# Softmax totals of the first attention layer: from 128x32 products in one bank to 64x64 products in two

## The chip, the cores and the metric

The kernel runs on one core of one Trainium2 chip. Its engines work side by side: TensorE (PE, with PEld for its weight loads), VectorE (DVE), ScalarE (ACT), GpSimd (POOL) and SyncE (SP), which here mostly issues transfers. [...] The metric is the device time of one execution in microseconds (us), as a median of several runs.

## The reference

The kernel computes two layers of attention over images, in fp32, for 8 images ("batches" here) of 512 channels and 32 x 32 = 1024 positions, with 8 heads of 64 channels. The part that matters is the first layer:

```python
x = x + L0(_gn(x))            # then a second attention layer on the result
# L0: group norm, then
qkv = einsum('oc,bct->bot', qkv_w, normed) + qkv_b
weight = einsum('bct,bcs->bts', q, k)          # q, k scaled by 64 ** -0.25
weight = softmax(weight, axis=-1)
a = einsum('bts,bcs->bct', weight, v)
out = einsum('oc,bct->bot', proj_w, xf + a) + proj_b
```

The second layer (head mixing, softmax, instance norm over each head's map) is not touched by the change.

## The kernel before

The kernel does layer 0 for all eight batches and then layer 1. The order of the instructions on each engine is the order in which the program writes them. Small pieces of work are put between the others with an `Agenda`: `ag.at(slot, fn)` files a function under a slot, and the main loop runs the slots as it comes to them.

In layer 0, each batch has projections for k, v and q (`project0`, matmuls at L899, in 128x128 of the PE array), then `attention0`, then the output projection. `attention0` works on 64 steps i = 0 to 63: 8 groups g of 8 steps. A group is one pair of heads (m = 0, 1) and one half of the queries (512 columns); a step is a block of 128 keys. The loop goes forward by two steps at a time:

- `scores(i)` (L1081): four products of 64x64 weights with 512 columns give the scores, keys on partitions, into two PSUM banks; then ACT takes the exponential into the tile `e` (L1086; 7 buffers).
- `values(i)` (L1107), two steps behind: four products of 64x64 with 512 columns. Keys 0 to 63 (a = 0) and keys 64 to 127 (a = 1) go to separate banks, the two heads to the halves of each bank. At the end of a group ACT copies the two banks out (`u`, L1118).
- `sums(i)` (L1092 and L1094): DVE adds the exponentials of the group into `zacc`, which still has 128 partitions of partial sums.
- Then come three stages of the softmax's division: `totals(g)` two slots after the group's last values, `reciprocals(g)` six slots after, `finish(g)` ten slots after.

`totals` adds `zacc` over its 128 partitions with products against ones (L1126), which also repeat each result over many partitions. ACT copies the result to SBUF (`row`, L1131), and a transfer on SP's queue spreads it over all 128 partitions, 8 values on each (`zc`, L1133). `reciprocals` adds the halves of `u` (L1137), inverts `zc` (L1140), sends the inverse to DRAM (L1142) and reads it back spread over the partitions (`rzb`, L1145). It also collects two numbers for a check of the range. `finish` multiplies `u` by `rzb` and adds it into `xa` (L1161, L1163).

Two more things have a part in this. PSUM has eight banks: layer 0 gives four to the score tiles (tag `s`), two to tag `a0`, one to `a1` and one to `small`. The tag `small` has one buffer and serves the group norm's statistics of the next batch, through `small_psum`. In batches 0 to 6 their first matmul (`gs.means`, L619, tile `pm`) is filed under slot 43, the second (`gs.squares`, L630, tile `pv`) under slot 45, and the reading of `pv` (`scale`) under slot 47:

```python
agenda.at(slot + 23, gs.means)      # slot = 20
agenda.at(slot + 25, gs.squares)
agenda.at(slot + 27, scale)
```

In batch 7 the statistics for layer 1 over batches 0 to 6 take the same bank, under slots 22, 25 and 28; the last of them begins with DVE's reading of `pv` (L634). With the loop's numbers, the totals of group g run in slot 8g + 10; those of group 7 run after the loop, behind the next projection's k (`ag.flush()`).

Of the kernel before, what the change touches and what calls it, by code (L numbers as in the profile page):

```python
# [9 lines left out]
F32 = mybir.dt.float32  # L10
# [8 lines left out]
P = 128  # L19
# [448 lines left out]
def tile_two_attention_layers(  # L468
# [19 lines left out]
    nc = tc.nc  # L488
    B, C, T = x_d.shape
    H = w_head.shape[0]  # L490
    D = C // H
    NCC = C // P
    NT = T // P
    FB = 512
# [21 lines left out]
    def const_tile(name, shape, dt=F32):  # L516
        return const.tile(shape, dt, tag=name, name=name)
# [13 lines left out]
    ones = const_tile("ones", [P, P])  # L531
# [162 lines left out]
    with ExitStack() as l0:  # L694
# [4 lines left out]
        zpool = l0.enter_context(tc.tile_pool(name="zpool", bufs=2))  # L699
        stat = l0.enter_context(tc.tile_pool(name="stat", bufs=2))  # L700
        ps_s = l0.enter_context(tc.tile_pool(name="ps_s", bufs=2, space=PSUM))
        ps_a = l0.enter_context(tc.tile_pool(name="ps_a", bufs=1, space=PSUM))

        def small_psum(nm):
            return ps_a.tile([P, FB], F32, tag="small", name=nm)
# [363 lines left out]
        def attention0(b, agenda):  # L1069
            q, k, v = q_t[b], k_t[b], v_t[b]  # L1070
            e, acc, u, zacc, zc, rzb = {}, {}, {}, {}, {}, {}
# [46 lines left out]
                        nc.scalar.copy(u[g][a], acc[g][a])  # L1118

            def totals(g):  # L1120


                HB = FB // 2
                z = ps_a.tile([P, FB], F32, tag="a0", name=f"z_{b}_{g}", bufs=2)[:, :HB]
                for c in range(4):
                    nc.tensor.matmul(  # L1126
                        z[c * 32 : c * 32 + 32], ones[:, :32], zacc[g][:, c // 2, ts(c % 2, HB)],
                        start=True, stop=True, tile_position=(0, c * 32),
                    )
                row = zpool.tile([P, HB], F32, tag="row", name=f"row0_{b}_{g}")  # L1130
                nc.scalar.copy(row, z)  # L1131
                zc[g] = stat.tile([P, T // P], F32, tag="zc", name=f"zc_{b}_{g}")
                nc.sync.dma_start(out=zc[g], in_=row[0::32])  # L1133

            def reciprocals(g):

                nc.vector.tensor_add(u[g][0], u[g][0], u[g][1])  # L1137
                zs = zc[g]
                rz = stat.tile([P, T // P], F32, tag="rz0", name=f"rz_{b}_{g}")
                nc.vector.reciprocal(rz, zs)  # L1140
                zd = dram.tile([2, FB], F32, tag=f"zd0_{b}_{g}", name=f"zd0_{b}_{g}")
                nc.sync.dma_start(out=zd, in_=rz)  # L1142
                rzb[g] = zpool.tile([P, FB], F32, tag="rzb", name=f"rzb_{b}_{g}")
                for m in range(2):
                    nc.sync.dma_start(  # L1145
                        out=rzb[g][m * D : m * D + D], in_=zd[m].partition_broadcast(D)
                    )
                col = b * H + g
                junk = stat.tile([P, T // P], F32, tag="junk0", name=f"junkz_{b}_{g}")
                nc.vector.tensor_scalar(  # L1150
                    junk, zs, 1.0, 0.0, ALU.mult, ALU.add, accum_out=chk[:, 1, col : col + 1]
                )
                r2 = stat.tile([P, T // P], F32, tag="r20", name=f"r2_{b}_{g}")
                nc.vector.scalar_tensor_tensor(
                    r2, rz, 1.0 / RZ_MAX, rz, ALU.mult, ALU.mult,
                    accum_out=chk[:, 0, col : col + 1],
                )
# [8 lines left out]
            for i in range(0, NI + 2, 2):  # L1166
                if i < NI:
                    scores(i)
                    scores(i + 1)
                if i >= 2:  # L1170
                    for w in (i - 2, i - 1):
                        values(w)
                        sums(w)
                    if (i - 1) % NG == NG - 1:
                        g = (i - 1) // NG
                        agenda.at(i + 2, lambda g=g: totals(g))
                        agenda.at(i + 6, lambda g=g: reciprocals(g))
                        agenda.at(i + 10, lambda g=g: finish(g))
                agenda.run(i)
                agenda.run(i + 1)  # L1180
# [83 lines left out]
    with ExitStack() as l1:  # L1264
# [5 lines left out]
        zpool = l1.enter_context(tc.tile_pool(name="zpool1", bufs=1))  # L1270
        stat = l1.enter_context(tc.tile_pool(name="stat1", bufs=2))
        ps_a = l1.enter_context(tc.tile_pool(name="ps1_a", bufs=2, space=PSUM))
# [619 lines left out]
        for b in range(B):  # L1892
            more = b + 1 < B
            a = Attention1(b)
# [143 lines left out]
```

## Time and profile before

| | us |
|---|---|
| median of three runs | 4051.75 |
| their range | 4051.15 to 4058.64 |
| profiled execution | 4059.13 |
| its span, first to last instruction | 4057.0 |
| PE busy | 3927.5 |
| DVE busy | 2834.4 |
| ACT busy | 1969.0 |
| POOL busy | 128.7 |

Layer 0 takes the time up to about 1750 us, layer 1 the rest. The mean granted clock of TensorE is 0.993 of full speed. In the profile, a row names the source line, the engine, the operation, the tiles (written <- read) and the shapes, then how many there were; a number in square brackets is how long the engine had been idle, with what ended that. A logical fp32 matmul is two matmuls in the trace, and matmuls in different parts of the PE array overlap.

### The profile page before, as it was taken

What the parts mean: (1) busy time and instruction counts of PE and PEld (TensorE: products, weight loads), DVE (VectorE), ACT (ScalarE), POOL (GpSimd) and SP (SyncE); (2) the same over time, 40 slices, a digit from 0 to 9 for tenths busy, and PEclk for the clock granted to TensorE, in tenths of its full rate; (3) what the DMA queues carried; (4) which work ended last, traced back from release to release, by engine and by line L of the source; (5) the groups of instructions that cost most, each with busy time, mean ns of one, the idle gap of its engine ahead of it and who ended that gap; (6) DMA issues with size and microseconds to landing.
All of it is one profiled execution on the core that took longest, in us unless ns stands there. A gap on an engine that the chain in (4) does not pass through costs nothing. (4 is left out here: it accounts for less than half of the span.)

```text
span 4057.0 us, 96037 instructions
## 1 busy us (share of the span) xinstructions
PE 3927.5 (97%) x41932; PEld 1817.7 (45%) x41932; DVE 2834.4 (70%) x4124; ACT 1969.0 (49%) x2431; POOL 128.7 (3%) x150
## 2 busy tenths in 40 slices
PE   8999999999999999999999999999999999999997
PEld 4353535353444435334444534544444444445344
DVE  4748475756666575748849859769679679498596
ACT  1727263545445363516617427347257166174273
POOL 0000000000000000000000001001000000000010
PEclk9999999999999999999999999999999999999998
DMA  3313131211111111228738639559469287386384
GB/s 124 114 47 115 45 118 48 87 50 59 60 66 66 68 53 60 77 83 208 182 120 220 189 105 234 155 143 231 128 174 233 78 216 194 114 223 193 104 212 121
DMA packets 268636, 519.12 MB, mean 128 GB/s; under 512 B 49840, under 2 KB 84912, under 8 KB 261552
## 3 DMA queue, kind: packets, MB, share of 16 engines
q1 hardware_dynamic: 261664, 497.96, 42.9%
q0 software_dynamic: 6544, 14.94, 1.6%
q8 instruction: 331, 5.42, 0.6%
q14 instruction: 97, 0.79, 0.1%
HBM read 197.16 MB, written 46.92 MB: 60 GB/s over the span
## 5 line engine op out<-in xcount | busy, mean ns | idle before, releaser
L1687 DVE STREAM_TRANSPOSE et<-e 128x2048 f32<-128x2048 f32 x256 | 586.7, 2292 | 133.8 <-ACT e L1675 127.6
L1714 PEld LDWEIGHTS a<-et,v 128*64 128x64 f32 x16384 | 509.4, 138 | 287.2 <-issue 215.8
L1698 DVE BATCH_NORM_STATS2 bn<-e 128x6 f32<-128x512 f32 x1024 | 633.5, 673 | 0.0
L1086 ACT ACTIVATE e<-s 128x1024 f32<-128x1024 f32 x512 | 497.2, 1026 | 233.9 <-PE s L1081 233.4
L1675 ACT ACTIVATE e<-m 128x1024 f32<-128x1024 f32 x512 | 496.3, 1021 | 208.4 <-issue 102.1
L1643 ACT COPY raw<-s 128x1024 f32<-128x1024 f32 x480 | 475.0, 1019 | 229.6 <-PE s L1631 193.1
L1714 PE MATMUL a<-et,v 128*64 128x64 f32 x16384 | 557.3, 225 | 5.8 <-DVE et L1687 5.1
L1631 PE MATMUL s<-k,q 64*64 64x512 f32 x4096 | 541.7, 615 | 9.7 <-DVE q L1497 3.1
L1094 DVE TENSOR_TENSOR zacc<-zacc,e 128x1024 f32<-128x1024 f32 x384 | 468.8, 1221 | 93.8 <-ACT e L1086 71.8
L1081 PE MATMUL s<-q,k 64*64 64x512 f32 x4096 | 490.1, 593 | 2.3 <-ACT e L1086 2.3
L1107 PE MATMUL a<-e,v 64*64 64x512 f32 x4096 | 484.1, 589 | 0.0
L1665 PE MATMUL m<-re,wmix 32*32 32x512 f32 x8192 | 334.9, 611 | 72.6 <-DMA re<-raw 60.7
L1107 PEld LDWEIGHTS a<-e,v 64*64 64x64 f32 x4096 | 156.7, 133 | 282.8 <-issue 282.5
L1081 PEld LDWEIGHTS s<-q,k 64*64 64x64 f32 x4096 | 147.9, 133 | 275.2 <-issue 240.7
L1631 PEld LDWEIGHTS s<-k,q 64*64 64x64 f32 x4096 | 118.0, 132 | 259.2 <-issue 85.0
L1458 PE MATMUL pv<-wv,y 128*128 128x512 f32 x480 | 212.1, 597 | 0.0
L1730 ACT COPY q<-a 64x256 f32<-64x256 f32 x256 | 93.7, 366 | 158.9 <-PE a L1714 156.3
L1665 PEld LDWEIGHTS m<-re,wmix 32*32 32x32 f32 x8192 | 71.6, 103 | 215.5 <-ACT raw L1643 88.3
L1763 POOL DMA_DIRECT2D zd<-rz x56 | 34.7, 619 | 3492.5 <-DMA y<-x 1858.2
L1458 PEld LDWEIGHTS pv<-wv,y 128*128 128x128 f32 x480 | 89.3, 190 | 117.4 <-issue 109.5
L1462 ACT COPY v<-pv 128x512 f32<-128x512 f32 x30 | 17.6, 585 | 218.4 <-PE pv L1458 218.4
L1092 DVE TENSOR_TENSOR zacc<-e,e 128x1024 f32<-128x1024 f32 x64 | 78.3, 1223 | 55.3 <-ACT e L1086 55.3
(315 smaller groups left out, 3936.8 us busy)
## 6 DMA issues: line engine op xcount, KB each, us to landing
re<-raw SPq DMA_DIRECT2D x1024, 256.0 KB
left_q<-left_q SPq DMA_DIRECT2D x17, 1792.0 KB
left_p<-left_p SPq DMA_DIRECT2D x17, 1792.0 KB
left_k<-left_k SPq DMA_DIRECT2D x10, 1792.0 KB
x<-in_x_dram SPq DMA_DIRECT2D x32, 512.0 KB
rzb<-zd SPq DMA_DIRECT2D x128, 128.0 KB
x<-x SPq DMA_DIRECT2D x64, 256.0 KB
left_v<-left_v SPq DMA_DIRECT2D x8, 1792.0 KB
```

Source lines behind the costliest of these rows:

```text
L1081: nc.tensor.matmul(ps[c * D : c * D + D, m], k[r, hp, k0 : k0 + D], q[r, hp, ts(f, FB)], start=True, stop=True,)
L1086: nc.scalar.activation(e[i], ps, AF.Exp, scale=S0 * S0)
L1094: nc.vector.tensor_add(zacc[g], zacc[g], e[i])
L1107: nc.tensor.matmul(acc[g][a][m * D : m * D + D], v[rows, kc, ts(2 * hp + m, D)], e[i][rows, m], start=(kc == 0), stop=(kc == NG - 1),)
L1458: nc.tensor.matmul(ps[:, m], y_t[b][:, c, ts(2 * i + m, P)], w[:, c], start=(c == 0), stop=(c == NCC - 1),)
L1631: nc.tensor.matmul(ps[c * D : c * D + D, m], qo_t[b][r, p, hp, ts(c, D)], k_t[b][r, hp, ts(kh, FB)], start=True, stop=True,)
L1643: nc.scalar.copy(dst, ps)
L1665: nc.tensor.matmul(ps[a // 2][c * 32 : c * 32 + 32, a % 2].rearrange("p (r kb k) -> p r kb k", r=2, k=32), wmix[rows].rearrange("p g i -> ...
L1675: nc.scalar.activation(e[:, :, 2 * h : 2 * h + 2].rearrange("p r a k -> p a r k"), ps[h].rearrange("p a (r k) -> p a r k", r=2), AF.Exp,)
L1687: nc.vector.transpose(self.et[p, u].rearrange("p kb (r st a) g q -> p st kb r (a g q)", r=2, st=2)[:, st], self.e[p, s].rearrange("p r a ( ...
L1698: nc.vector.bn_stats(self.bn[p][:, s, a], e[:, :, a].rearrange("p r k -> p k r"))
L1714: nc.tensor.matmul(acc[two * D : two * D + D, s].rearrange("p (x q) -> p x q", q=4), v_t[b][:, kb, ts(g, D)], et[:, kb, :, g], start=(kb = ...
```

## The change

The products of `totals` become four of 64x64 weights with 512 columns: per key half a and head m one, the halves in separate banks, a = 0 in a bank of tag `a0` as before and a = 1 in the bank of tag `small`. So each total arrives as two halves. Two copies on ACT, of 128x512 each, take the place of one of 128x256; two transfers take the place of one; `row` has one buffer of 2 x 512 columns instead of two of 256; and DVE adds the two halves of `zc`, 128x8 elements, ahead of the reciprocal.

```diff
             def totals(g):
-                HB = FB // 2
-                z = ps_a.tile([P, FB], F32, tag="a0", name=f"z_{b}_{g}", bufs=2)[:, :HB]
-                for c in range(4):
-                    nc.tensor.matmul(
-                        z[c * 32 : c * 32 + 32], ones[:, :32], zacc[g][:, c // 2, ts(c % 2, HB)],
-                        start=True, stop=True, tile_position=(0, c * 32),
-                    )
-                row = zpool.tile([P, HB], F32, tag="row", name=f"row0_{b}_{g}")
-                nc.scalar.copy(row, z)
-                zc[g] = stat.tile([P, T // P], F32, tag="zc", name=f"zc_{b}_{g}")
-                nc.sync.dma_start(out=zc[g], in_=row[0::32])
+                z = [ps_a.tile([P, FB], F32, tag="a0", name=f"z_{b}_{g}", bufs=2), small_psum(f"zs_{b}_{g}")]
+                for a in range(2):
+                    rows = slice(a * D, a * D + D)
+                    for m in range(2):
+                        nc.tensor.matmul(
+                            z[a][m * D : m * D + D], ones[rows, :D], zacc[g][rows, m],
+                            start=True, stop=True,
+                        )
+                row = zpool.tile([P, 2, FB], F32, tag="row", name=f"row0_{b}_{g}", bufs=1)
+                zc[g] = stat.tile([P, 2, T // P], F32, tag="zc", name=f"zc_{b}_{g}")
+                for a in (1, 0):
+                    nc.scalar.copy(row[:, a], z[a])
+                    nc.sync.dma_start(out=zc[g][:, a], in_=row[0::D, a])

             def reciprocals(g):
                 nc.vector.tensor_add(u[g][0], u[g][0], u[g][1])
-                zs = zc[g]
+                zs = zc[g][:, 0]
+                nc.vector.tensor_add(zs, zs, zc[g][:, 1])
                 rz = stat.tile([P, T // P], F32, tag="rz0", name=f"rz_{b}_{g}")
```

## The prediction

> **What bounds the kernel.** I read the page's busy times first, then windows one softmax group long, then the timelines of the places where the totals are made. The profiled execution took 4059.13 us, 4057.0 of them span; the median of the runs shown is 4051.75, lower by 7.4 us, about their own spread (4051.15 to 4058.64). I make the sum against the profile and add it to the median.
>
> ```profile
> PE 3927.5 (97%) x41932; PEld 1817.7 (45%) x41932; DVE 2834.4 (70%) x4124; ACT 1969.0 (49%) x2431; POOL 128.7 (3%) x150
> ```
>
> ```profile
> 129.96:144.42 14.46, 14.46 (x141) 4.95 (x137) 9.19 (x14) 11.55 (x17) 0.00 (x0) 1.00 0.37 147
> 329.57:344.04 14.47, 14.47 (x141) 4.96 (x137) 14.09 (x23) 9.82 (x12) 0.00 (x0) 1.00 0.24 77
> ```
>
> Each window runs from one totals matmul to the next (length, then PE, PEld, DVE, ACT busy): PE is busy throughout, DVE 9.2 to 14.1, ACT 9.8 to 11.6 of 14.5 us. So the first layer's attention is paced by PE. What lengthens PE's stream there counts in full; ACT, DVE and DMA count only if they make PE wait.
>
> A busy PE says little about the price of an instruction, so I take prices from starts:
>
> ```profile
> 113.67 1.90 PE L1107 MATMUL a<-e,v 64*64 64x512 f32 x16
> 115.49 0.64 PE L1126 MATMUL z<-zacc,ones 128*32 128x256 f32 x8
> 116.06 1.95 PE L1081 MATMUL s<-q,k 64*64 64x512 f32 x16
> 117.83 1.90 PE L1107 MATMUL a<-e,v 64*64 64x512 f32 x16
> 119.55 1.90 PE L1081 MATMUL s<-q,k 64*64 64x512 f32 x16
> 121.26 1.04 PE L1107 MATMUL a<-e,v 64*64 64x512 f32 x8
> ```
>
> Without totals, 16 matmuls of 64x512 take 121.26 - 119.55 = 1.71 to 1.72 us: four run side by side and a new set of four starts every 0.429 us. From 113.67 to 117.83 are 4.16 us, two such stretches (3.43) and the totals, so the totals cost PE 0.73 us. Two sets of 256 columns are by length 2 x 0.215 = 0.43 of that. The other 0.30 are gaps at the changes between 64*64 and 128*32: z starts 0.11 later than 113.67 + 1.72, s another 0.14 later than 0.43 after z, and s's first set takes 0.05 more.
>
> The Trainium skill, page "TensorEngine Tiling (Array Packing)", section "Tiling Modes", says that changing the tiling mode, not only the tile, drains TensorE. The 0.30 us agree. The same page's "Restrictions and Gotchas" says that row tiles must not write one PSUM bank at the same time; L1107 already keeps to that, with one bank per row half, and its sets of four start 0.429 apart. The new products have L1107's shape and bank layout, so the forecast goes by L1107's row.
>
> **Part 1: the products.** Away: two sets in 128*32 and both mode changes, 0.73 us. Added: four logical products of 64x64x512, in fp32 two matmuls each like L1107's, so 8 matmuls = two sets = 2 x 0.429 = 0.86 us, with no mode change between `values` and `scores`. Net +0.13 us per group. Six groups of each of the 8 batches (48) stand so, without a further wait: 48 x 0.13 = +6.2 us. Bounds: 0.09 to 0.20 each, 4.3 to 9.6.
>
> **Part 2: the `small` bank.** This is the step that I weigh most. `zs` takes the one buffer of tag `small`, which the next batch's group statistics use too. In 7 batches `gs.means` (slot 43) issues its matmul right behind the totals of group 4 (slot 42), so this matmul now waits until ACT has copied `zs`:
>
> ```profile
> 387.43 0.64 PE L1126 MATMUL z<-zacc,ones 128*32 128x256 f32 x8
> 388.00 0.39 PE L619 MATMUL pm<-gs_m,gavg 128*128 128x4 f32 x2
> 388.31 1.95 PE L1081 MATMUL s<-q,k 64*64 64x512 f32 x16
> ```
>
> ```profile
> 388.13 0.37 ACT L1131 COPY row<-z 128x256 f32<-128x256 f32 x1 [1.08 <-PE z L1126]
> 389.47 1.94 ACT L1086 ACTIVATE e<-s 128x1024 f32<-128x1024 f32 x2 [0.96 <-PE s L1081]
> ```
>
> ACT idles before the copy, so the copy starts as z ends. Let X be when PE could start the totals (387.32 here). Before: z at X + 0.11, pm at X + 0.68. After: sets at X and X + 0.43, a set lasts 0.61 (two last 1.04 in the row of 121.26, less 0.43), so the last ends at X + 1.04; ACT starts 0.06 later and copies 128x512 in 0.59 (L1118's mean, 589 ns): X + 1.69; the release takes some 0.06 more, so pm is at about X + 1.75. That is +1.07, part 1 included. The scores behind pm on PE, and all else, move with it. 7 x 1.07 = +7.5 us. Bounds: 0.6 if part of the copy is hidden, 1.6 if pm also waits for the second copy: 4.2 to 11.2.
>
> In the last batch it is the other way round: the statistics over batches 0 to 6 write `pv` at slot 25 and read it at slot 28, and totals of group 2 (slot 26) lie between. `zs` must wait for that read, which stands on DVE behind two additions for slot 26's exponentials:
>
> ```profile
> 1644.44 0.64 PE L1126 MATMUL z<-zacc,ones 128*32 128x256 f32 x8
> 1645.01 1.95 PE L1081 MATMUL s<-q,k 64*64 64x512 f32 x16
> ```
>
> ```profile
> 1643.56 2.55 DVE L1094 TENSOR_TENSOR zacc<-zacc,e 128x1024 f32<-128x1024 f32 x2
> 1646.02 0.18 DVE L634 COPY gs_var<-pv 128x28 f32<-128x28 f32 x1
> ```
>
> The read ends at 1646.20; two half-filled sets of zs take 0.86; scores start near 1647.1 instead of 1645.01: once +2.1 us. Bounds 1.2 to 3.5, since DVE itself waits there for a reciprocal's transfer.
>
> **Part 3: the last group.** Group 7's totals run in 128*128 surroundings, between projections, so mode changes stay:
>
> ```profile
> 236.61 0.64 PE L1126 MATMUL z<-zacc,ones 128*32 128x256 f32 x8
> 237.52 7.17 PE L899 MATMUL pv_p<-left_v,n 128*128 128x256 f32 x32 [0.28 <-DVE k L955]
> ```
>
> z's sets grow from 0.43 to 0.86, but 0.28 of that lies in a wait that PE has anyway; with 0.11 for the change of mode pv starts at 236.61 + 0.97 = 237.58, +0.06. 7 x 0.06 = +0.4 us. In the last batch the wait is 0.64 and hides all. Bounds: 0 and the whole 0.43 in each: 0 to 3.
>
> **Part 4: what I cost at nothing.** ACT: two copies of 128x512 (1.07 us overlapped, as L1118's pair shows at other groups) for one of 0.37, +0.70 per group. What hides it: behind the first group's totals the pair of exponentials ends at 119.16, and the scores that reuse the second one's bank start at 119.55 + 0.86 = 120.41, 1.25 later; where ACT comes to the copy late (groups 2 and 3, behind the statistics' passes) that slack is 1.13 and 0.94. In the usual group the copies end some 0.2 past the time at which the next exponential could start, in groups 2 and 3 the full 0.70; at least 0.2 us stay. Without that cover it would be up to 0.70 x 64 = 45 us. SP: a second zc transfer, 0.59 us of issue. It is issued at about X + 2.2 and lands 1.84 after its issue starts (237.71 to the reciprocal at 239.55), X + 4.1; the reciprocal comes at X + 6.0 or later. Behind it on SP are x and left loads, needed many us later; POOL's queue has no part in this layer's groups (0.00 in the windows). `row` has one buffer instead of two, but its last reader was issued a group, 14 us, before. Where the left loads run (group 3, reciprocal late by up to 1.5 us) it lands with them. DVE: one addition of 128x8, near 0.11 to 0.20 us (the rows of the same size), plus the wait; its lag behind the exponentials reaches 4 us, and e has 7 buffers, 5.9 us to spare at the worst. Group 7's chain (copies, both transfers, reciprocal, broadcast) lengthens by about 1.3 us; DVE then idles 2.13 us before the addition that PE needs, in one batch 0.7, and PE needs it only 1.9 us later.
>
> **Sum.** 6.2 + 7.5 + 2.1 + 0.4 = +16.2 us, on the span 4057.0 to 4073; on the median 4051.75 to 4068.0 (+0.40%). The ends of the bounds add to +9.7 and +27.3.
>
> **Rivals.** About 0.2%, 8.1 us, is what a measurement of this kernel tells from no change.
> - *The bank waits cost next to nothing*: only parts 1 and 3 remain, +6.6, 4058.4: within 0.2%. For it: pm is a tiny matmul, and the copy of `zs` is put first to free the bank. Against: PE issues in order, and pm follows z directly. Chance 0.12.
> - *Faster*: the mode changes also keep neighbouring sets from overlapping more than the starts show, so that without them the eight matmuls run partly inside their neighbours' sets. At 0.30 per group, 56 x (0.30 - 0.73) = -24, and the bank waits give back about 9: -15, 4036. It passes -0.2% from 0.43 us per group downward. Against: sets of four of this very shape are 0.429 apart everywhere. Chance 0.04.
> - *ACT becomes the bound*: the copies eat the 0.94 to 1.25 us of slack and scores wait for their bank. At 0.3 per group, 64 x 0.3 = 19 us more: 4087. Against: 2.9 us of free ACT in the fullest window. Chance 0.10.
> - The change does what it says, with the arithmetic untouched; the remaining 0.74 is my case.
>
> Hence faster 0.04, same 0.13, slower 0.83. The range reaches down to the first rival, 4058, and up to nearly the upper sum of the bounds (4079): 4058 to 4078.
>
> **What would show it.** PE: z and zs as 64*64 64x512, scores 0.86 after z, group period 14.59 instead of 14.46; pm some 1.75 us behind z's start, waiting for ACT row; near the slot of L634 a wait of PE for DVE of about 2 us; ACT row x128, about 45 us more busy; no longer waits of scores for e. Wrong it is if the period shrinks, if pm follows z at 0.9, or if scores wait for ACT in the usual group.

## The result, and the profile after

| | before | after |
|---|---|---|
| median, us | 4054.36 (4051.15 to 4058.64, 6 runs) | 4073.69 (4067.38 to 4077.69, 6 runs) |
| ratio to before | 1 | 1.0047 [1.0034, 1.0060] |
| span of the profiled execution, us | 4057.0 | 4075.8 |

The changed kernel is slower by about 19 us. The first line is of its page; the two windows again run from one totals matmul to the next, with the length and then the busy times of PE, PEld, DVE and ACT.

```profile
PE 3941.3 (97%) x41932; PEld 1838.6 (45%) x41932; DVE 2843.2 (70%) x4188; ACT 2010.7 (49%) x2495; POOL 128.6 (3%) x150
```

```profile
129.15:143.74 14.59, 14.59 (x140) 5.20 (x136) 8.88 (x14) 12.04 (x18) 0.00 (x0) 1.00 0.38 146
330.58:345.17 14.59, 14.59 (x140) 5.20 (x136) 14.18 (x24) 10.56 (x13) 0.00 (x0) 1.00 0.22 66
```

A group takes 14.59 us, 0.13 more than before, and PE is still busy throughout. The timeline of PE at the first totals (start, duration, operation) shows why:

```profile
112.84 1.90 PE L1107 MATMUL a<-e,v 64*64 64x512 f32 x16
114.56 0.59 PE L1125 MATMUL z<-zacc,ones 64*64 64x512 f32 x1
114.56 0.59 PE L1125 MATMUL zs<-zacc,ones 64*64 64x512 f32 x1
...
115.42 1.90 PE L1081 MATMUL s<-q,k 64*64 64x512 f32 x16
117.13 1.90 PE L1107 MATMUL a<-e,v 64*64 64x512 f32 x16
```

From 112.84 to 114.56 are 1.72 us, the length of 16 matmuls, so z begins without a gap, and the scores begin 0.86 later: two full sets of four, no mode change. Behind the totals of group 4 the next batch's statistics wait for the bank, here in PE's and ACT's timelines of batch 1:

```profile
388.94 0.59 PE L1125 MATMUL z<-zacc,ones 64*64 64x512 f32 x1
...
390.05 0.58 ACT L1132 COPY row<-zs 128x512 f32<-128x512 f32 x1 [1.37 <-PE zs L1125]
390.53 0.59 ACT L1132 COPY row<-z 128x512 f32<-128x512 f32 x1
...
390.69 0.39 PE L619 MATMUL pm<-gs_m,gavg 128*128 128x4 f32 x2 [0.71 <-ACT row L1132]
391.00 1.95 PE L1081 MATMUL s<-q,k 64*64 64x512 f32 x16
```

`pm` starts 1.75 us after z, when the first copy has ended and not the second. In batch 7 the stall is much longer:

```profile
1657.25 1.03 PE L1125 MATMUL z<-zacc,ones 64*64 64x512 f32 x4
1661.88 0.65 PE L1125 MATMUL zs<-zacc,ones 64*64 64x512 f32 x2 [3.61 <-DVE gs_var L634]
1661.90 0.66 PE L1081 MATMUL s<-q,k 64*64 64x512 f32 x2
1662.37 0.60 PE L1125 MATMUL zs<-zacc,ones 64*64 64x512 f32 x2
1662.38 3.03 PE L1081 MATMUL s<-q,k 64*64 64x512 f32 x12
```

z takes its two sets with half the array, and zs stands 4.63 us behind it, waiting for DVE's read at L634. DVE's own timeline says why that read is late (the bracket: idle before, and what ended it):

```profile
1657.85 0.69 DVE L1162 TENSOR_TENSOR u<-u,rzb 128x512 f32<-128x512 f32 x1 [3.61 <-DMA rzb<-zd]
1658.58 0.69 DVE L1164 TENSOR_TENSOR xa<-xa,u 128x512 f32<-128x512 f32 x1
1659.19 2.55 DVE L1094 TENSOR_TENSOR zacc<-zacc,e 128x1024 f32<-128x1024 f32 x2
1661.65 0.18 DVE L634 COPY gs_var<-pv 128x28 f32<-128x28 f32 x1
```

In DVE's stream `finish` of group 1 (the first two rows) stands before the read. It waited 3.61 us for `rzb`, the reciprocal that comes back from DRAM; before the change it waited 0.89 us at this place:

```profile
1642.22 0.69 DVE L1161 TENSOR_TENSOR u<-u,rzb 128x512 f32<-128x512 f32 x1 [0.89 <-DMA rzb<-zd]
```

The stall has a second cost. Two windows of 3.41 us of the changed kernel, the first up to 1662.95 and the second from there; the third number from the end is TensorE's granted clock:

```profile
1659.54:1662.95 3.41, 1.06 (x12) 0.52 (x16) 3.13 (x10) 0.00 (x0) 0.00 (x0) 1.00 0.00 0
1662.95:1666.36 3.41, 3.41 (x24) 1.37 (x17) 2.59 (x13) 2.14 (x4) 0.00 (x0) 0.50 0.04 2
```

Just after the restart PE ran at half clock for 3.41 us, which cost it 1.71 us; the trace of the kernel before has no such stretch in layer 0's attention. Being 4.63 us late and losing 1.71 make 6.34 us. Group 2 to 3 takes 20.13 us instead of 14.59, and the stretch from group 6's to group 7's totals 34.61 instead of the other batches' 33.78: together 6.37 more.

Counted between z's starts, 7 batches take 13.5 us more and batch 7 7.4 us more (g0 to g7: 128.70 against 121.32). What lies before the first totals and after the last is 2.0 us shorter in this execution, though the change touches nothing there. 13.48 + 7.38 - 2.01 = 18.85 us, the difference of the spans.

### The profile page after: what moved, and what is told of

It reads as the page before. It is cut to its first block, busy times and chain, and to the rows that moved or that the text cites. A ratio compares the mean times of both kernels' runs of the same rounds, so it can differ in the third digit from the quotient of the medians.

```text
span 4075.8 us, 96335 instructions
## 1 busy us (share of the span) xinstructions
PE 3941.3 (97%) x41932; PEld 1838.6 (45%) x41932; DVE 2843.2 (70%) x4188; ACT 2010.7 (49%) x2495; POOL 128.6 (3%) x150
## 5 line engine op out<-in xcount | busy, mean ns | idle before, releaser
L1081 PE MATMUL s<-q,k 64*64 64x512 f32 x4096 | 504.2, 592 | 2.3 <-ACT e L1086 2.3
L1107 PE MATMUL a<-e,v 64*64 64x512 f32 x4096 | 500.0, 590 | 0.0
L1081 PEld LDWEIGHTS s<-q,k 64*64 64x64 f32 x4096 | 159.8, 133 | 279.6 <-issue 245.4
L899 PE MATMUL pv_p<-left_v,tmp 128*128 128x256 f32 x512 | 113.1, 379 | 0.0
```

The source lines that it names most:

```text
L1081: nc.tensor.matmul(ps[c * D : c * D + D, m], k[r, hp, k0 : k0 + D], q[r, hp, ts(f, FB)], start=True, stop=True,)
L1107: nc.tensor.matmul(acc[g][a][m * D : m * D + D], v[rows, kc, ts(2 * hp + m, D)], e[i][rows, m], start=(kc == 0), stop=(kc == NG - 1),)
```

## The experiments

The theory: the loss is PE's longer stream in every group (0.13), plus two waits made by the shared bank `small`: `pm` behind zs in 7 batches, and zs behind the read of `pv` in batch 7. A rival puts the loss on ACT, DVE or the transfers, which would stay when the bank is free. A second question is what of the old 0.73 us was gaps at the mode changes.

**The bank made free (e1_stats_moved)**, and the same moves in the kernel before as control (e3_before_moved). `gs.means` goes behind other work, and batch 7's statistics are read before the totals come:

```diff
-            agenda.at(slot + 23, gs.means)
-            agenda.at(slot + 25, gs.squares)
+            agenda.at(slot + 25, gs.means)
+            agenda.at(slot + 26, gs.squares)
...
-                for slot, fn in zip((22, 25, 28), group_stages(0, B - 1, small_psum)):
+                for slot, fn in zip((21, 23, 24), group_stages(0, B - 1, small_psum)):
```

> The changed kernel, with the group statistics filed so that they no longer meet the totals in the bank of tag small: in batches 0 to 6 the first statistics matmul goes from slot 43 to 45 and the second from 45 to 46; in batch 7 the three stages go from slots 22, 25, 28 to 21, 23, 24. My theory (the excess over the old kernel is 0.13 us for each of 56 groups, plus 7 waits of pm for ACT's copy of about 1.06 less 0.13, plus one wait of some 5.5 us in batch 7, plus 0.1 in each of 7 last groups): the waits go, about 12 us of the changed kernel's 19 are taken back, 4062 or +0.2% on the old kernel is left, and every group in the loop takes 14.59 us or less. Rival (the 64x64 products or the two copies themselves are dearer than the starts show, and the waits only shift idle time): less than 4 us come back.

> The old kernel with the same moves of the statistics (slots 45 and 46, and 21, 23, 24), as the control. My theory: there the statistics meet no totals in their bank, so the move does nothing: 4054, within 0.1% of the old kernel. Rival: the move is worth something of its own, by 5 us or more either way; then the first experiment's gain isn't the waits' alone.

Measured: e1 4063.46 us, ratio to before 1.0023 [1.0014, 1.0033]; e3 4056.17 us, 0.9999 [0.9990, 1.0007]. So the moves alone change the total by less than 0.1%, and with the bank free the loss is halved. In e1's timeline of PE, `pm` follows `values` with no wait:

```profile
391.12 1.90 PE L1107 MATMUL a<-e,v 64*64 64x512 f32 x16
392.94 0.39 PE L619 MATMUL pm<-gs_m,gavg 128*128 128x4 f32 x2
393.26 1.95 PE L1081 MATMUL s<-q,k 64*64 64x512 f32 x16
```

A batch takes 215.25 us (before 214.08, after 216.02), and batch 7 lasts 122.32 from g0 to g7 (121.32 and 128.70). 7 x 1.17 + 1.0 = 9.2 us is left over before, where the ratio says 9.3. Some 1.2 of them are the moves' own: in e3 a batch takes 214.25, 0.17 more than before. Against e3 the new totals cost 1.00 us per batch, 8.0 in all: seven groups of 0.13 and one tenth at the last. The rival falls: with ACT's, DVE's and SP's added work all in place, what remains is PE's own stream.

**Half the columns (e4_half_columns).** The new products with 256 columns instead of 512 (the totals of half the queries are left out), the copies as large as in the changed kernel. PE's length is then the old one, without the mode changes:

```diff
-                            z[a][m * D : m * D + D], ones[rows, :D], zacc[g][rows, m],
+                            z[a][m * D : m * D + D, : FB // 2], ones[rows, :D], zacc[g][rows, m, : FB // 2],
...
-                    nc.scalar.copy(row[:, a], z[a])
+                    nc.scalar.copy(
+                        row[:, a].rearrange("p (r c) -> p r c", r=2),
+                        z[a][:, : FB // 2].unsqueeze(1).to_broadcast([P, 2, FB // 2]),
+                    )
```

> The changed kernel with products of 64x64x256 instead of 64x64x512: the totals of the second 256 queries are left out (the copies take the first 256 twice, so ACT and the transfers have the same work as in the changed kernel). It has as many columns per set as the old kernel's products and no change of tiling mode. My theory (0.43 of the old 0.73 us are columns, 0.30 are the two mode changes): totals cost PE 0.43 us in a group, 0.43 less than in the changed kernel, so with 64 groups about 27 us less: 4046, or 0.2% under the old kernel. Rival (the 0.30 us are not the mode changes but the wait for the semaphore or the reading of ones and zacc, which are the same here): 0.73 per group, 0.13 less than in the changed kernel, about 8 us less: 4065.

Measured: 4056.95 us, 1.0003 [0.9994, 1.0011]. As a total this hits neither theory. The timeline of PE does decide:

```profile
125.93 1.90 PE L1107 MATMUL a<-e,v 64*64 64x512 f32 x16
127.64 0.38 PE L1125 MATMUL z<-zacc,ones 64*64 64x256 f32 x1
...
128.07 1.90 PE L1081 MATMUL s<-q,k 64*64 64x512 f32 x16
```

The scores come 0.43 after z, and the group takes 14.16 us instead of 14.46: the pair of mode changes cost 0.30 us. The copies and transfers are as many and as large as in the changed kernel, so they are not what sets its 14.59 either. My total left out the waits, which did not shrink with the matmuls: group 4 to 5 takes at best 15.89 us (before 15.25, as `pm` still waits for a full copy, 1.32 behind z), and group 2 to 3 of batch 7 takes 20.93 (before 14.46). Four batches keep 1.00 us each of the 1.8 that six groups could bring, two keep 0.7 and 0.4, and batch 6, where `pm` waits 1.84 us for DVE, loses 1.8. That leaves 3.3 us, and batch 7's stall takes 6.5. Around the end of both of these waits the clock was at half, for 3.41 us in batch 6 and 6.83 in batch 7.

**The other copy first (e6_small_last).** If `pm` waits for the copy that frees the bank, then copying z first delays it by one copy's length.

```diff
-                for a in (1, 0):
+                for a in (0, 1):
```

> The changed kernel, with the two copies in the other order: z of tag a0 first, zs of tag small second. My theory (pm waits for just the copy that frees small): in the group with pm (group 4 of batches 0 to 6) pm starts about 0.48 us later, 2.2 us behind z's start instead of 1.74, 3.4 us in all 7; the groups without pm keep 14.59 us. Rival (pm waits for PE's own drain or for ACT being busy with exponentials): pm stays at 1.74.

Measured, one execution: 4080.28 us, span 4078.5.

```profile
388.66 0.59 PE L1125 MATMUL z<-zacc,ones 64*64 64x512 f32 x1
...
390.86 0.38 PE L619 MATMUL pm<-gs_m,gavg 128*128 128x4 f32 x2 [1.16 <-ACT row L1132]
```

`pm` is 2.20 us behind z instead of 1.75, group 4 to 5 takes 16.77 us instead of 16.32, and the groups without `pm` stay at 14.59. So the order of two copies sets this wait. In batch 7 the stall happened to be smaller (17.27 against 20.13 us, DVE waiting 2.44 for `rzb`). The span's +2.7 is therefore not the sum of these two (7 x 0.45 - 2.9 = 0.3): what lies behind the last totals, which the edit leaves as it is, took 3.5 us longer in this execution than in the changed kernel's.

**The loads that stand before the reciprocal (e5_y_later).** In batch 7 SP's queue of the changed kernel reads:

```profile
1643.38 1.18 SPq L1133 DMA_DIRECT2D zc<-row  x2
1644.65 1.84 SPq L1229 DMA_DIRECT2D y<-x  x4
1648.38 0.32 SPq L1143 DMA_DIRECT2D zd<-rz  x1
1653.04 1.15 SPq L1146 DMA_DIRECT2D rzb<-zd  x2
```

Four loads of y stand between group 1's totals and its reciprocal. In the kernel before they do too, but they are issued 1.79 us after that group's z instead of 2.99:

```profile
1630.09 0.59 SPq L1133 DMA_DIRECT2D zc<-row  x1
1630.77 1.84 SPq L1228 DMA_DIRECT2D y<-x  x4
1635.15 0.32 SPq L1142 DMA_DIRECT2D zd<-rz  x1
1638.77 1.10 SPq L1145 DMA_DIRECT2D rzb<-zd  x2
```

Against that z (1628.98 before, 1641.66 after) `zd` is issued 0.55 later, `rzb` follows `zd` after 4.66 instead of 3.62, and DVE gets it 4.81 after its issue starts instead of 3.45: 2.95 us in all. If the y loads cause that, moving them behind the read-back takes the stall away and leaves the bank as it is:

```diff
-                ag.at(20, load_first)
+                ag.at(23, load_first)
```

> The changed kernel, with the four loads of y (2 MB) in batch 7 filed under slot 23 instead of 20, so that they stand behind the read-back of group 1's reciprocals (rzb) on SP's queue and no longer ahead of it. My theory on the stall of 5.5 us at group 2 of batch 7 (forecast 2.1): zs waits for DVE's reading of pv (L634), which stands in DVE's queue behind finish of group 1, and that waits 3.61 us for rzb, landing behind the y loads. Then DVE's wait for rzb goes, L634 runs some 1 us after z's start instead of 4.4, and the stall of group 2 falls from 5.5 to 2 us or less. Rival (DVE is late there by its own additions): the stall stays at 4 us or more.

Measured, one execution: 4073.15 us, span 4071.3, 4.5 below the changed kernel's.

```profile
1656.72 1.03 PE L1125 MATMUL z<-zacc,ones 64*64 64x512 f32 x4
1658.16 0.65 PE L1125 MATMUL zs<-zacc,ones 64*64 64x512 f32 x2 [0.41 <-DVE gs_var L634]
```

```profile
1653.64 0.69 DVE L1162 TENSOR_TENSOR u<-u,rzb 128x512 f32<-128x512 f32 x1
1657.92 0.18 DVE L634 COPY gs_var<-pv 128x28 f32<-128x28 f32 x1
```

DVE no longer waits for `rzb`, zs follows z after 1.44 us instead of 4.63, group 2 to 3 takes 15.23 us instead of 20.13, and the clock stays at full there. The bank makes the dependency; the transfers ahead of the reciprocal make it long. How y loads issued 1.20 us later become 2.95 us at DVE was not taken apart.

**Mode changes shared (e7_paired, e8_paired_pm).** Since a pair of mode changes costs 0.30 us, the kernel before gains if one visit to 128x32 serves two groups. Each half of one bank of tag `a0` takes one group's totals; `zacc` and `u0` get a third buffer, and `u` is added before the totals arrive. e7 pairs groups (0,1), (2,3), (4,5); e8 pairs (1,2), (3,4), (5,6), so that `pm` shares a visit as well.

```diff
+                for n, g in enumerate(gs):
+                    for c in range(4):
+                        nc.tensor.matmul(
+                            z[c * 32 : c * 32 + 32, ts(n, HB)], ones[:, :32],
+                            zacc[g][:, c // 2, ts(c % 2, HB)],
+                            start=True, stop=True, tile_position=(0, c * 32),
+                        )
...
+                        elif g % 2:
+                            agenda.at(i + 2, lambda g=g: totals(g - 1, g))
```

> The old kernel's 128x32 products, but the totals of groups 0 and 1, 2 and 3, 4 and 5 taken together in one visit of PE to that tiling mode, in the two halves of one bank of tag a0 (one copy on ACT for both, a third buffer for zacc and u0, the addition of u1 ahead). My theory: one pair of mode changes serves two groups, so a visit costs 0.30 + 0.86 = 1.16 us instead of 2 x 0.73, 0.30 less for each of 24 pairs: 7 us less than the old kernel, 4047, or 0.17% under it. Rival (the gap belongs to each set of products, not to the mode change): no change, 4054. DVE does its divisions in two neighbouring slots; if it falls behind by more than the 7 buffers of e can take, the kernel gets slower.

> As the paired kernel, but pairs of groups 1 and 2, 3 and 4, 5 and 6, so that the visit for 3 and 4 comes directly ahead of pm and shares a mode change with it, as in the old kernel. In the first pairing the visits cost what I expected (28.63 us for two groups instead of 28.93), but pm, standing alone, cost 0.2 us more in each of 7 batches, and a batch took 213.47 instead of 214.08. My theory: that 0.2 comes back, a batch takes 213.2, and the whole is 7 us under the old kernel (0.17%), 4048. Rival (the gain is lost elsewhere, in DVE's bursts): as the first pairing, within 0.1% of the old kernel.

Measured: e7 4052.33 us, 0.9995 [0.9987, 1.0003]; e8 4050.99 us, 0.9995 [0.9988, 1.0001]. Both totals fall short of what I expected. The visit itself is as forecast (e7's timeline of PE):

```profile
127.05 1.90 PE L1107 MATMUL a<-e,v 64*64 64x512 f32 x16
128.88 1.07 PE L1126 MATMUL z<-zacc,ones 128*32 128x256 f32 x16
129.88 1.95 PE L1081 MATMUL s<-q,k 64*64 64x512 f32 x16
```

Sixteen matmuls, 1.00 us from z to the scores, and two groups in 28.63 us where they took 28.93: 0.30 saved per pair. A batch takes 213.47 us in e7 and 213.38 in e8 (before 214.08). In e8 batch 7 gives some of it back, as PE's and DVE's timelines show:

```profile
1667.87 0.64 PE L1126 MATMUL z<-zacc,ones 128*32 128x256 f32 x8
1670.25 0.64 PE L1126 MATMUL z<-zacc,ones 128*32 128x256 f32 x8 [1.74 <-DVE zacc L1094]
```

```profile
1663.05 0.69 DVE L1165 TENSOR_TENSOR u<-u,rzb 128x512 f32<-128x512 f32 x1 [6.65 <-DMA rzb<-zd]
```

The second half of the visit waits for `zacc`, because DVE stood 6.65 us for a reciprocal behind another large load on SP. After that wait of PE too the clock was at half for 3.41 us, and the pair took 32.28 us.

**Those loads moved too (e9_paired_left)**, with the same move in the kernel before (e10_left_later):

```diff
-                ag.at(32, lambda: load_left("k", b + 1))
-                ag.at(33, lambda: load_left("v", b + 1))
+                ag.at(37, lambda: load_left("k", b + 1))
+                ag.at(37, lambda: load_left("v", b + 1))
```

(and so for batch 7's `load_left("q1", 0)` and `load_left("k1", 0)`)

> The second paired kernel (groups 1 and 2, 3 and 4, 5 and 6), with the loads of the next weights (left, 2 x 1.8 MB) filed under slot 37 instead of 32 and 33, behind the read-back of group 2's reciprocals on SP's queue. In its trace a batch took 213.38 us, 0.70 less than in the old kernel, where 0.90 was expected, and in batch 7 PE waited 1.7 us for zacc because DVE had stood 6.65 us for rzb behind these loads. My theory: that is where the pairing's gain went; with the loads later the batch takes 213.2, the wait in batch 7 goes, and the whole is some 7 us (0.17%) under the old kernel, 4048. Rival (the gain is eaten by waits all over): as the paired kernels, within 0.1% of the old kernel.

> The old kernel with the same move of the weight loads to slot 37, as the control. My theory: the old kernel's PE does not wait for these loads, so nothing changes: 4055, within 0.1%. Rival: the move alone gives a gain of 3 us or more, and then the gain of the experiment beside it isn't the pairing's.

Measured: e9 4050.50 us, 0.9987 [0.9979, 0.9994], which beats both kernels by a little; e10 4109.41 us, 1.0130 [1.0115, 1.0146]. In e9 the wait in batch 7 is gone (28.63 us for the pair), but a batch still takes 213.38, so the 0.2 us that I hoped to get back there stayed lost. e10 was foreseen by neither side. Its waits of PE (total, times, longest) and DVE's and SP's timelines of batch 1:

```profile
PE pm L619 <- DVE gs_m L617: 39.7, 8, 6.0
```

```profile
398.69 0.69 DVE L1161 TENSOR_TENSOR u<-u,rzb 128x512 f32<-128x512 f32 x1 [7.72 <-DMA rzb<-zd]
```

```profile
381.97 0.46 SPq L740 DMA_DIRECT2D left_k<-left_k  x1
382.49 0.42 SPq L740 DMA_DIRECT2D left_v<-left_v  x1
385.63 0.32 SPq L1142 DMA_DIRECT2D zd<-rz  x1
395.07 1.11 SPq L1145 DMA_DIRECT2D rzb<-zd  x2
```

The two loads now stand just ahead of group 3's read-back. DVE waits 7.72 us for it, `gs_m` stands behind that on DVE, and PE waits for `gs_m`. From 398.56 on the clock is at half:

```profile
400.25 0.59 PE L619 MATMUL pm<-gs_m,gavg 128*128 128x4 f32 x2 [5.96 <-DVE gs_m L617]
```

```profile
398.56:405.39 6.83, 5.14 (x26) 2.04 (x30) 5.60 (x10) 1.89 (x2) 0.00 (x0) 0.50 0.00 0
```

Group 4 to 5 takes 23.46 us in batch 0 and 23.76 in batch 1 instead of 15.25, some 8 us more, and so in each of the 7 batches. In batch 1 it is 8.51: 5.96 of waiting, and half of the 5.14 us that were left of the slow stretch when PE went on. In e9 the same slot is harmless, since there the queue is free of read-backs: the loads go out at 369.72 and 370.31, and the next transfer of totals at 387.21. So e10 is no clean control of the pairing. It shows that the slot alone brings no gain. e8 and e9, which differ in the move alone, tell the two apart: a batch takes 213.38 us in both, so the 0.70 per batch is the pairing's, and the move only ends batch 7's wait (28.63 us for the pair instead of 32.28). These are timelines of one execution each.

## Why the prediction was right, and where a term was off

It gave 4068.0 us, +16.2 on the sum, and slower as the likely side. The medians measured together lie 19.3 apart, the spans 18.8. All its terms but one came out in mechanism and, nearly, in size; the one for batch 7 was far too small.

*Part 1, the products: right.* 0.86 from z to the scores and 14.59 per group, as forecast. The Trainium skill's rule ("TensorEngine Tiling (Array Packing)", section "Tiling Modes"), that a change of mode drains TensorE, stood beside 0.30 us of gaps in the trace before; e4 (14.16 against 14.46) and e7 (28.63 against 28.93) measured the same 0.30 twice. They also say why dropping the mode changes did not pay: it saves 0.30 and doubles 0.43 us of columns.

*Part 2, `pm`: right.* 1.75 behind z was forecast, 1.75 measured, and group 4 to 5 grew by 1.07. With parts 1 and 3 the forecast has 0.78 + 1.07 + 0.06 = 1.91 per batch; 1.94 was measured. The reason given (the copy of zs, in front of z's) is confirmed by e6 and e1.

*Part 2, batch 7: right in mechanism, mis-sized.* It took DVE's read of `pv` where it stood in the trace before and gave 2.1 us, at most 3.5. Measured are 6.5: group 2 to 3 takes 20.13 us instead of 14.46, and the stretch to group 7's totals is 0.83 longer than in e1, which has no stall (34.61 against 33.78). Two things make the difference of 4.4.

The first is the read. By the forecast zs could start 1.9 us behind the totals' start; it started 4.63 behind. The prediction named DVE's wait for a reciprocal there, but kept its old length. Part 4 had counted the second zc transfer and said that only loads needed later stand behind it. It did not look at what stands behind *those*: the read-back of group 1's reciprocal, which DVE needs before the read that releases zs. So 2.95 us of delay on the queue went into the very wait that the step had to size; e5 shows, by moving only the y loads, that these make it long.

The second is the clock, for which the prediction has no term: at half for 3.41 us after the stall, 1.7 us lost. 2.7 and 1.7 are the 4.4. The same sum, zs's lateness and the time lost to the clock, fits the other runs with a stall there: 1.44 against 1.47 measured in e5, 3.47 against 3.51 in e6, 4.91 + 2.27 against 7.17 in e4.

*Part 3, group 7: right.* pv starts 1.02 after z instead of 0.91, one tenth against 0.06, and nothing in batch 7.

*Part 4, no cost: right for PE.* ACT's busy time rose by 41.7 us (forecast 45), the addition of the zc halves takes 0.16 us, and the scores' waits for ACT's exponentials stayed (in total 2.3 us for PE in both traces; for the weight loads 24.9 before, 25.8 after). Only the transfers' lateness surfaced, at the one place where a wait was already open.

*Rivals.* "The bank waits cost next to nothing" is refuted by the 0.71 us bracket at `pm` and by e1, which gains half the loss from freeing the bank. The faster case needed sets closer than 0.429; the eight matmuls took 0.86. ACT as the bound would have left its loss in e1, and would not have let e4's groups run in 14.16 us.

The median lies 5.7 above the forecast. Of that, 2.6 is the median of before itself, which stood higher with more runs (4054.36 instead of 4051.75). In the spans the forecast is 2.6 short: batch 7's excess of 4.5, less the 2.0 us by which the stretches outside happened to be shorter. That offset is chance, and the total came out nearer than its batch-7 term deserved.

## What to carry to other kernels

Price an instruction on a full engine from the spacing of starts, and price a shared PSUM buffer by asking who uses it next and behind which copy or read that user will stand. When a wait on another engine sets the price, don't take that engine's old times: follow its queue back through the transfers, since a small read-back behind large loads can be late by several us (DVE waited 7.72 for one in e10). Look at the granted clock behind every long wait of PE: in four of these runs a stall cost more than its length. A pair of mode changes of the array (0.30 us here) is worth sharing between visits, and worth avoiding only if that does not lengthen the products by more than the change costs.

## What the runs showed of the hardware that was not expected

- In layer 0's attention the granted clock was at half in eleven stretches, of 3.41 or 6.83 us, all in four of the runs: one in the changed kernel, two in e4, one in e8 and seven in e10. Each began around the end of a wait of PE of 1.74 us or more. A wait of 2.44 us in e6 had none, so the length of the wait alone does not tell, and what sets it off was not tried.
- After the stall in batch 7 the scores of one row half start (1661.90) before zs's second set (1662.37), which stands ahead of them in the program. From then on zs starts 0.85 us behind z instead of beside it, two sets of four, until the attention ends. The group keeps its 14.59 us, but the stretch to group 7's totals, where full-array matmuls follow, is 0.83 us longer. e5 and e6 have the same 0.85 and 34.61 us, with shorter stalls; e1, without one, has 33.78. In e4, whose totals have half the columns, zs is 0.42 behind and the stretch 0.40 longer (33.76 against 33.36 in its other batches). So the cost goes with the skew of the two row halves in all of them; an edit that changes the skew alone was not tried.
- Moving two loads behind one small transfer and ahead of the next cost 1.3% of the kernel (e10), though the bytes moved and the instructions of all engines stayed the same.
